# Folding the third hop's weights into the first hop's product, and turning its sums on VectorE

## Chip, cores and metric

The program runs on one core of a Trainium2 chip. A core has TensorE (PE in the profile; its weight loads are PEld), VectorE (DVE), ScalarE (ACT), GpSimd (POOL), SyncE (SP, which here only issues transfers) and 16 DMA engines. The metric is the device time of one execution in microseconds. The median of three runs of the kernel before is 697.6 us (697.42 to 697.65).

## What is computed

A stack of four graph layers works on node vectors `x` of 3327 nodes by 64 features and one dense-stored adjacency `adj` of 3327 x 3327, all float32. Each layer is `x = x + layer(relu(layernorm(x)), adj)`. Cut to what matters here:

```python
# layer 0: two gated cells, each m = adj @ (h @ W), then gates (sigmoid, tanh)      hops 0, 1
# layer 1: a rank-weighted mask of adj times (h @ weight) + bias                     hop 2
# layer 2: w = adj * adj; three hops with a dense layer each                         hops 3, 4, 5
for W, b in ((W0, b0), (W1, b1), (W2, b2)):
    x = w @ x
    x = x @ W.T + b
# layer 3: twice x = tanh(concat(adj @ x, x) @ W[k])                                 hops 6, 7
```

So there are eight products with an N x N matrix. The change concerns layer 2. A product from the right with the small matrices commutes with the products with `w` from the left, so `W0`, `W1` and `W2` may be applied at any one of the three hops, as long as each bias goes through the matrices that follow it: `b0` is still multiplied by `w` twice, `b1` once.

## The kernel before

**Tiling.** The nodes are padded to 26 blocks of 128. Blocks are paired (block b and block 13 + b stand in the two 64-row halves), which gives 13 pairs in four chunks: chunks 0, 1 and 2 have three pairs (384 columns), chunk 3 has four (512). Chunks 0 and 1 are group 0; chunks 2 and 3 are group 1. An adjacency tile is one source block (26 of them) by one group. A unit of work is one hop, one chunk and one tile: two matmuls into the two halves of a PSUM bank (L613). The records show four instructions for each, since a float32 product is recorded as two.

**Order of the hops.** `joint(g, k, ...)` at L661 writes down the order of units for hop k and hop k+1 of one group, so that a tile loaded once serves both. The call `joint(1, 4)` does hops 4 and 5 of group 1, then `joint(0, 5)` hops 5 and 6 of group 0, then `joint(1, 6)`. Within one, tiles of the other group's nodes come first; hop k+1 follows hop k by four tiles (`later=4`). The group's own tiles come next. The last `sweep` of them are done for the first chunk completely, then for the second, so that the first chunk's sums are finished early. Then the waiting tiles of hop k+1 are done, then hop k+1 over the first chunk's own sources for both chunks, then over the second chunk's own sources for the first chunk, and for the second.

**Tasks.** What follows a chunk's last unit (evacuation, dense layer, layernorm) is a Python generator, `after_k`. Nothing in it is dynamic on the chip: while the program is written out, every unit "spends" a time (0.645 for a 384-column chunk, 0.86 for 512, L617), and a generator that has yielded a time is continued when that time is spent. So a `yield` sets only after which unit the next instructions are put into the engines' queues. `begin` for a chunk first runs the chunk's old task to its end (`finish`, L372), and a unit that reads a node vector which its task has not yet set runs that task to its end (L603). The task of loading and folding constants, `more_constants`, ends with `fold_hops` (L228), which multiplies `W0` and `W1` into one matrix (`product(1, 2)`).

**Hop 5 before.** `after_5` (L1013) copies the sums to SBUF (`evacuate`: VectorE for even chunks, ScalarE for odd), multiplies them with `W2` on TensorE (`dense_to_nodes`, which at the same time brings them from feature layout to node layout), adds the result to `x` from PSUM (`residual`), normalises (`layernorm_relu`), and after 8.0 writes the transposed vector into `both[c]` with 16 VectorE transposes (`transpose_on_vector`) for the concatenation of hop 6. `b2` was added to `x` long before, by `add_row(c, 2)` at the end of `after_2`. Hop 4 already has no dense product: `sums_to_nodes` (L813) adds a bias column on ScalarE and turns the sums with 16 VectorE transposes of 32-row blocks.

**Squares.** Hops 3 to 5 need `adj * adj`. In `joint(0, 5)` the tile itself is still needed by hop 6, so each unit squares its part into a separate half slot, three units ahead (`expand`, L490). `square` (L444) chooses the engine: ScalarE, except that every third square goes to VectorE when no chunk has a task alive.

**After hop 6.** `after_6` (L1025) copies the sums into the free halves of `both[c]`, one half on ScalarE (L830), one on VectorE (L834), and 1.3 later TensorE multiplies `both` with layer 3's weights (`stacked_to_nodes`, L780).

Of the kernel before, what the change touches and what calls it, by code (L numbers as in the profile page):

```python
# [9 lines left out]
F32 = mybir.dt.float32  # L10
# [3 lines left out]
ALU = mybir.AluOpType  # L14
# [30 lines left out]
N, D = 3327, 64  # L45
P = 128
# [9 lines left out]
GROUPS = [(0, 1), (2, 3)]  # L56
# [9 lines left out]
WL1, WL2, WL3 = 14, 15, 18  # L66
# [25 lines left out]
def upper(n):  # L92
    return slice(n * D, (n + 1) * D)
# [3 lines left out]
def kernel(  # L97
# [9 lines left out]
    nc = tc.nc  # L107
# [3 lines left out]
    work = ctx.enter_context(tc.tile_pool(name="work", bufs=4))  # L111
# [11 lines left out]
    bd = const.tile([P, 4, P], F32, name="bd")  # L123
# [7 lines left out]
    brow = const.tile([P, 4, D], F32, name="brow")  # L131
    hopcol = const.tile([P, 2], F32, name="hopcol")
    ident = const.tile([P, P], F32, name="ident")
    make_identity(nc, ident)
    tri = const.tile([P, P], BF16, name="tri")
    behind = const.tile([P, NQ - 1 + D], BF16, name="behind")
# [77 lines left out]
    def product(i, j):  # L214

        n, ps = take()
        mm(ps[:, :P], bd[:, i, :], ident)
        tr = work.tile([P, P], F32, name="t2")
        nc.scalar.copy(tr, ps[:, :P])
        give(n)  # L220
        yield 1.0
        n, ps = take()
        mm(ps[:, :P], tr, bd[:, j, :])
        nc.scalar.copy(bd[:, i, :], ps[:, :P])
        give(n)
        yield 1.0

    def fold_hops():  # L228

        i, ps = take()  # L230
        for n in range(3):
            for h in range(2):
                nc.tensor.matmul(ps[upper(h), n * P:(n + 1) * P], brow[:, n], ident, start=True, stop=True)
        cols = work.tile([P, CWM], F32, name="t2")
        nc.scalar.copy(cols[:, :3 * P], ps[:, :3 * P])
        give(i)
        yield 1.0

        i, ps = take()
        mm(ps[:, :D], cols[:, :P], bd[:, 2, :D])  # L240
        nc.vector.tensor_copy(brow[:, 0], ps[:, :D])
        nc.vector.tensor_copy(hopcol[:, 0:1], cols[:, P:P + 1])
        give(i)
        yield 1.0
        yield from product(1, 2)

    def more_constants():
# [54 lines left out]
    def blocks(c):  # L302
        return CH[c][1] - CH[c][0]

    def width(c):
        return blocks(c) * P

    def mm(out, lhsT, rhs, start=True, stop=True):


        for h in range(2):
            hs = slice(h * D, (h + 1) * D)
            nc.tensor.matmul(out[hs], lhsT[:, hs], rhs, start=start, stop=stop)  # L313
# [8 lines left out]
    def take(sums=False, either=True):  # L322


        either = either and not sums
        pool = idle_sums if sums else idle_temps
        if either and idle_sums and (not pool or released[idle_sums[0]] < released[pool[0]]):
            pool = idle_sums
        for c in list(tasks):
            if not pool and c not in running:  # L330
                advance(c)
        i = pool.popleft()
        return i, banks[i]

    def give(i):
        released[i] = max(released) + 1
        (idle_sums if i < 4 else idle_temps).append(i)

    def nodes(c):

        return feat.tile([P, blocks(c), 2, D], F32, name=f"y{c}")

    def flat(t):
        return t.rearrange("p b s d -> p b (s d)")
# [4 lines left out]
    def xchunk(c):  # L349
        return xs[:, CH[c][0]:CH[c][1]]  # L350
# [8 lines left out]
    def advance(c):  # L359
        running.add(c)  # L360
        try:
            tasks[c][1] = next(tasks[c][0])
        except StopIteration:
            del tasks[c]
        running.discard(c)
# [6 lines left out]
    def finish(c):  # L372
        while c in tasks:
            advance(c)
# [14 lines left out]
    y = [[None] * NC for _ in range(8)]  # L389
# [233 lines left out]
    def put(k, c, t):  # L623
        units.append((k, c, t))
        if k == COUNT or KIND[k] != RANKED or c == GROUPS[t.g][0]:
            t.uses += 1
# [34 lines left out]
    def joint(g, k, sweep, later, keep, lag=None):  # L661


        a, b = GROUPS[g]
        in_place = KIND[k] != PLAIN and KIND[k + 1] == SQUARED
        early = (KIND[k], KIND[k + 1]) == (PLAIN, RANKED)
        waiting = deque()
        counting = Counting(g, lag)

        def both(t):  # L670
            for c in (a, b):
                put(k, c, t)
            if lag is not None:
                counting.add(t)

        def second(n):
            for _ in range(n):
                if waiting:
                    t = waiting.popleft()
                    for c in (a, b):  # L680
                        put(k + 1, c, t)

        for q in sources_of(*GROUPS[1 - g]):
            t = Tile(q, g, in_place, early)
            both(t)
            waiting.append(t)
            if len(waiting) > later:
                second(1)
        own = [[Tile(q, g, in_place, early) for q in sources_of(c)] for c in (a, b)]
        all_own = own[0] + own[1]  # L690
        for n, t in enumerate(all_own[:-sweep]):
            both(t)
            second(len(waiting) + n + 1 > later if early else min(2, len(waiting) - keep))
        counting.rest()
        for c in (a, b):
            for t in all_own[-sweep:]:
                put(k, c, t)
                if lag is not None and c == a:
                    counting.add(t)
            if KIND[k] == RANKED:  # L700
                units.append((k, c, SPECIAL))
        counting.rest()
        second(len(waiting))
        for t in own[0]:
            for c in (a, b):
                put(k + 1, c, t)
        for c in (a, b):
            for t in own[1]:
                put(k + 1, c, t)
            if KIND[k + 1] == RANKED:  # L710
                units.append((k + 1, c, SPECIAL))
# [44 lines left out]
    def evacuate(acc, c, busy=False):  # L756
        m = work.tile([P, CWM], F32, name="t2")[:, :width(c)]
        if c % 2 or busy:
            nc.scalar.copy(m, acc[0][1][:, :width(c)])
        else:  # L760
            nc.vector.tensor_copy(m, acc[0][1][:, :width(c)])  # L761
        give(acc[0][0])
        return m

    def dense_to_nodes(ft, w, c):

        i, ps = take()
        v = view(ps, c)
        for b in range(blocks(c)):
            mm(v[:, b, :], ft[:, b * P:(b + 1) * P], bd[:, w - WL1, :])  # L770
        return i, v
# [38 lines left out]
                if q % 2:  # L810
                    yield 1.5

    def sums_to_nodes(acc, c, bias):  # L813

        m = work.tile([P, CWM], F32, name="t2")[:, :width(c)]
        nc.scalar.activation(m, acc[0][1][:, :width(c)], AF.Identity, bias=hopcol[:, bias:bias + 1])  # L816
        give(acc[0][0])
        yield 0.8
        v = m.rearrange("p (b q n) -> p b q n", q=4, n=32)
        yk = nodes(c)  # L820
        for s in range(2):
            for f in range(2):
                at = s * D + f * 32
                for q in range(4):
                    nc.vector.transpose(yk[q * 32:(q + 1) * 32, :, s, f * 32:(f + 1) * 32], v[at:at + 32, :, q])  # L825
                yield 1.2
        return yk
# [33 lines left out]
    def residual(v, c, relu=False):  # L861
        if relu:
            nc.vector.scalar_tensor_tensor(flat(xchunk(c)), v[1], 0.0, flat(xchunk(c)), op0=ALU.max, op1=ALU.add)
        else:
            nc.vector.tensor_tensor(flat(xchunk(c)), flat(xchunk(c)), v[1], ALU.add)  # L865
        give(v[0])

    def add_row(c, i):

        n = 2 * blocks(c)  # L870
        nc.vector.tensor_tensor(groups(xchunk(c)), groups(xchunk(c)),
                                brow[:, i:i + 1, :].to_broadcast([P, n, D]), ALU.add)
# [113 lines left out]
    def after_2(c, acc):  # L986
        m = evacuate(acc, c)
        yield 1.4
        v = dense_to_nodes(m, WL1, c)
        yield 1.2  # L990
        residual(v, c)
        yk = nodes(c)
        yield from layernorm_relu(yk, c, squares_on_scalar=c in GROUPS[0])
        y[3][c] = yk
        yield 15.0
        add_row(c, 2)

    def after_3(c, acc):
        m = evacuate(acc, c)
# [11 lines left out]
        y[5][c] = yield from sums_to_nodes(acc, c, 0)  # L1011

    def after_5(c, acc):  # L1013
        m = evacuate(acc, c)
        yield 0.8
        v = dense_to_nodes(m, WL2 + 2, c)
        yield 0.8
        residual(v, c)
        yk = nodes(c)
        yield from layernorm_relu(yk, c)  # L1020
        y[6][c] = yk
        yield 8.0
        yield from transpose_on_vector(yk, c)
# [31 lines left out]
    joint(1, 2, sweep=6, later=6, keep=1)  # L1055
    joint(0, 3, sweep=8, later=4, keep=4)
    joint(1, 4, sweep=8, later=4, keep=4)
    joint(0, 5, sweep=8, later=4, keep=4)
    joint(1, 6, sweep=8, later=4, keep=4)
    alone(0, 7, sweep=6, parts=True)  # L1060

# [55 lines left out]
```

## Time and profile before

| | us |
|---|---|
| median of three runs | 697.6 |
| the profiled execution's own time | 697.73 |
| its span, first to last instruction | 695.7 |
| TensorE busy | 681.0 (98%) |
| VectorE busy | 355.3 (51%) |
| ScalarE busy | 274.3 (39%) |
| GpSimd busy | 77.8 (11%) |

Times in the trace count from the start of the span. In a row of a group, the number behind "x" is how many instructions it has, then come their busy time in us and the mean of one in ns, then the idle time of the engine ahead of them and what ended it. In the chain, a row is start, length and the engine with the written tile and the line. In a timeline, a row is start, length, engine, line, operation, output and input with shapes, and in brackets the idle time ahead of it.

The 16 DMA engines moved 201.31 MB in the span, 289 GB/s on average.

### The profile page before, as it was taken

The page shows a single profiled execution, that of the slowest core. Times are in us where ns is not written, and L with a number is a line of the kernel's source. Part 1 is how long each engine was busy: PE and PEld are TensorE (multiplying, and loading weights), DVE is VectorE, ACT ScalarE, POOL GpSimd, SP SyncE. Part 2 cuts the span into 40 slices and gives each one's busy share as a digit, 9 for nine tenths or more (in the row PEclk, how much of TensorE's full clock was granted, in tenths as well). Part 3 has the DMA queues.
Part 4 walks back from the last instruction along what each step waited for, and adds up shares of the span by engine and source line. Part 5 has one row for each costly group of instructions (what it writes and reads, how often), then busy time and mean ns, then how long its engine had stood idle before and what let it go on. Part 6 is the DMA issues. An engine that isn't in the chain of part 4 may idle for free.

```text
span 695.7 us, 12589 instructions
## 1 busy us (share of the span) xinstructions
PE 681.0 (98%) x5072; PEld 380.4 (55%) x5072; DVE 355.3 (51%) x772; ACT 274.3 (39%) x426; POOL 77.8 (11%) x114
## 2 busy tenths in 40 slices
PE   7899999999999999999999999999999999999997
PEld 4686667645566785556444444343344444344587
DVE  5946745755997899757341106325271565005101
ACT  1013000403147878888998107722176500000101
POOL 5300000002480414111100000000000000000000
PEclk9999999999999999999999999999999999999999
DMA  9999998099879921792899569954997399917991
GB/s 341 401 400 406 403 407 274 1 349 389 277 242 376 317 96 60 259 316 80 311 361 351 206 216 409 404 227 131 396 370 264 110 399 405 405 75 268 404 403 65
DMA packets 68693, 201.31 MB, mean 289 GB/s; under 512 B 7244, under 2 KB 8372, under 8 KB 68636
## 3 DMA queue, kind: packets, MB, share of 16 engines
q1 hardware_dynamic: 65724, 199.08, 76.9%
q10 hardware_dynamic: 736, 1.23, 0.5%
q8 instruction: 40, 0.66, 0.4%
q0 software_dynamic: 2176, 0.20, 0.2%
q14 instruction: 17, 0.14, 0.0%
HBM read 199.45 MB, written 0.85 MB: 288 GB/s over the span
## 4 chain that ended last, share of the span: by engine, by line
PE 58%; DVE 1%; ACT 0%; POOL 0%; issue 0%; DVEq 0%; ACTq 0%; POOLq 0%
PE sum L613 54%; PE temp L313 3%; PE temp L780 1%; ACT e L529 0%; POOL st L854 0%; DVE both L834 0%; DVE e L527 0%; PE sum L313 0%; ACT both L830 0%; DVE y L858 0%; DVE y L850 0%; DVE t L845 0%; DVE st L851 0%; DVE st L843 0%; DVE xs L865 0%
## 5 line engine op out<-in xcount | busy, mean ns | idle before, releaser
L613 PE MATMUL sum<-adj,y 128*64 128x384 f32 (+3 forms) x3016 | 535.4, 501 | 1.5 <-DVE y L858 0.7
L613 PEld LDWEIGHTS sum<-adj,y 128*64 128x64 f32 x3016 | 248.8, 137 | 230.5 <-issue 196.9
L446 ACT ACTIVATE adj<-adj 128x768 f32<-128x768 f32 (+1 forms) x176 | 144.4, 892 | 45.9 <-PE sum L613 23.0
L472 DVE TENSOR_SCALAR adj<-adj 128x768 bf16<-128x768 f32 (+3 forms) x208 | 114.0, 597 | 32.6 <-PE temp L548 24.7
L613 PE MATMUL sum<-e,both 128*64 128x384 bf16 (+1 forms) x624 | 74.0, 339 | 0.5 <-DVE e L527 0.5
L529 ACT ACTIVATE e<-temp,bitsb 128x384 int16<-128x384 f32 (+1 forms) x120 | 67.8, 607 | 14.9 <-PE temp L313 9.1
L830 ACT COPY both<-sum 64x384 f32<-64x384 f32 (+3 forms) x17 | 8.1, 478 | 148.2 <-PE sum L613 148.2
L834 DVE COPY both<-sum 64x384 f32<-64x384 f32 (+3 forms) x13 | 7.3, 561 | 99.5 <-ACT both L830 98.9
L448 DVE TENSOR_TENSOR adj<-adj 128x768 f32<-128x768 f32 (+1 forms) x32 | 30.6, 1004 | 51.9 <-DMA adj<-in_adjT 33.1
L854 POOL TENSOR_TENSOR st<-st,mhalf 128x6 f32<-128x6 f32 (+1 forms) x16 | 24.9, 1553 | 287.8 <-DVE st L852 287.8
L313 PE MATMUL temp<-adj,tri 128*64 128x384 bf16 (+1 forms) x332 | 51.7, 341 | 1.3 <-ACT e L529 0.8
L613 PEld LDWEIGHTS <-both 128*64 128x64 bf16 x624 | 41.9, 110 | 18.3 <-issue 6.5
L477 POOL DMA_DIRECT2D adj<-totals x52 | 33.6, 648 | 52.6 <-PE temp L313 41.7
L313 PEld LDWEIGHTS <-tri 128*64 128x64 bf16 x416 | 29.2, 110 | 17.3 <-issue 9.8
L527 DVE TENSOR_SCALAR e<-temp 128x384 int16<-128x384 f32 (+1 forms) x46 | 28.3, 615 | 20.0 <-PE temp L313 9.6
L809 DVE STREAM_TRANSPOSE both<-y 32x96 f32<-32x96 f32 (+1 forms) x128 | 35.6, 278 | 2.9
L548 PE MATMUL temp<-adj,behind 128*64 128x384 bf16 x208 | 33.8, 340 | 2.8 <-DVE adj L472 2.6
L825 DVE STREAM_TRANSPOSE y<-t 32x96 f32<-32x96 f32 (+1 forms) x64 | 17.8, 278 | 24.7 <-ACT t L816 23.9
L548 PEld LDWEIGHTS <-behind 128*64 128x64 bf16 x208 | 20.8, 110 | 17.4 <-issue 13.5
L761 DVE COPY t<-sum 128x384 f32<-128x384 f32 x6 | 3.3, 555 | 35.7 <-PE sum L613 35.7
L186 ACT COPY t<-temp 128x128 f32<-128x128 f32 x1 | 0.3, 266 | 48.2 <-PE temp L184 48.2
L570 POOL MEMSET adj<- 128x768 f32 (+1 forms) x2 | 1.6, 800 | 133.2 <-PE sum L613 133.2
(132 smaller groups left out, 353.8 us busy)
## 6 DMA issues: line engine op xcount, KB each, us to landing
adj<-in_adjT SPq DMA_DIRECT2D x130, 768.0 KB, 9.0
adj<-in_adjT SPq DMA_DIRECT2D x104, 896.0 KB, 12.0
xs<-in_x ACTq DMA_DIRECT2D x1, 448.0 KB
adj<-totals POOLq DMA_DIRECT2D x26, 3.0 KB, 4.9
adj<-totals POOLq DMA_DIRECT2D x26, 3.5 KB, 2.3
out<-xs ACTq DMA_DIRECT2D x1, 256.0 KB
xs<-in_x SPq DMA_DIRECT2D x1, 192.0 KB
xs<-in_x ACTq DMA_DIRECT2D x1, 192.0 KB, 3.3
```

The costliest lines, as they stand in the source:

```text
L313: nc.tensor.matmul(out[hs], lhsT[:, hs], rhs, start=start, stop=stop)
L446: nc.scalar.activation(sq, v, AF.Square)
L448: nc.vector.tensor_tensor(sq, v, v, ALU.mult)
L472: nc.vector.tensor_scalar(t.mask.view[:rows, half], t.view()[:rows, half], 0.0, None, op0=ALU.not_equal)
L477: nc.gpsimd.dma_start(out=t.mask.view[P - 1:P], in_=totals[t.g][t.q:t.q + D + 1:D, :])
L527: nc.vector.tensor_scalar(wide[:, s], ps[:, :w], BITS, 0.0, op0=ALU.add, op1=ALU.max)
L529: nc.scalar.activation(wide[:, s], ps[:, :w], AF.Relu, bias=bitsb)
L548: nc.tensor.matmul(counts[c][1][s * D:(s + 1) * D, :w], behind[:, NQ - 1 - t.q:NQ - 1 - t.q + D], t.mask.view[:, s, t.cols(c)], start=firs ...
L613: nc.tensor.matmul(acc[h][1][h * D:(h + 1) * D, :w], yq[h], rhs[h], start=first and n == 0, stop=last and n == len(terms) - 1)
L809: nc.vector.transpose(to[at:at + 32, :, q], h[q * 32:(q + 1) * 32, :, s, f * 32:(f + 1) * 32])
L825: nc.vector.transpose(yk[q * 32:(q + 1) * 32, :, s, f * 32:(f + 1) * 32], v[at:at + 32, :, q])
L854: nc.gpsimd.tensor_tensor(st[:, 3, :n], st[:, 2, :n], mhalf[:, :n], ALU.pow)
```

## The change

The three matrices of layer 2 are folded into one at the start, `W0.T @ W1.T @ W2.T` (a second `product`), which hop 3's dense product applies. `b0`'s row goes through `W1` and `W2`, `b1`'s column through `W2`, and `b2` becomes a column of its own. Hop 5 then needs no product: like hop 4, it adds a bias column on ScalarE and turns the sums on VectorE, and adds the result to `x` from SBUF. `add_row` for `b2` goes. In hop 5 the second chunk of a group issues its turns only once the first chunk's normalised vector is set (the loop with `yield 0.3`, at most 50 times). In `joint(0, 5)` the sweep is 12 instead of 8: all twelve own tiles of group 0 are done for chunk 0 first, then for chunk 1.

```diff
         mm(ps[:, :D], cols[:, :P], bd[:, 2, :D])
+        mm(ps[:, D:D + 1], bd[:, 3, :], cols[:, P:P + 1])
         nc.vector.tensor_copy(brow[:, 0], ps[:, :D])
-        nc.vector.tensor_copy(hopcol[:, 0:1], cols[:, P:P + 1])
+        nc.vector.tensor_copy(hopcol[:, 0:1], ps[:, D:D + 1])
+        nc.vector.tensor_copy(hopcol[:, 1:2], cols[:, 2 * P:2 * P + 1])
         give(i)
         yield 1.0
+        i, ps = take()
+        for h in range(2):
+            nc.tensor.matmul(ps[upper(h), :P], brow[:, 0], ident, start=True, stop=True)
+        col = work.tile([P, P], F32, name="t2")
+        nc.scalar.copy(col, ps[:, :P])
+        give(i)
+        yield 1.0
+        i, ps = take()
+        mm(ps[:, :D], col, bd[:, 3, :D])
+        nc.vector.tensor_copy(brow[:, 0], ps[:, :D])
+        give(i)
+        yield 1.0
+        yield from product(2, 3)
         yield from product(1, 2)
...
-    def sums_to_nodes(acc, c, bias):
+    def sums_to_nodes(acc, c, bias, behind=None):
...
         yield 0.8
+        for _ in range(50):
+            if behind in (None, c) or y[6][behind] is not None:
+                break
+            yield 0.3
+        else:
+            finish(behind)
         v = m.rearrange("p (b q n) -> p b q n", q=4, n=32)
...
         y[3][c] = yk
-        yield 15.0
-        add_row(c, 2)
...
-        m = evacuate(acc, c)
-        yield 0.8
-        v = dense_to_nodes(m, WL2 + 2, c)
-        yield 0.8
-        residual(v, c)
-        yk = nodes(c)
+        yk = yield from sums_to_nodes(acc, c, 1, behind=GROUPS[c // 2][0])
+        nc.vector.tensor_tensor(flat(xchunk(c)), flat(xchunk(c)), flat(yk), ALU.add)
         yield from layernorm_relu(yk, c)
...
-    joint(0, 5, sweep=8, later=4, keep=4)
+    joint(0, 5, sweep=12, later=4, keep=4)
```

## Prediction

> **What bounds the kernel now.** I read the page first (busy times, slices of the span), then the groups of instructions with their shapes kept apart.
>
> ```profile
> span 695.7 us, 12589 instructions
> ...
> PE 681.0 (98%) x5072; PEld 380.4 (55%) x5072; DVE 355.3 (51%) x772; ACT 274.3 (39%) x426; POOL 77.8 (11%) x114
> ...
> PE   7899999999999999999999999999999999999997
> ...
> L825 DVE STREAM_TRANSPOSE y<-t 32x96 f32<-32x96 f32 x48 | 12.9, 270 | 22.1 <-ACT t L816 21.4
> ...
> L313 PE MATMUL temp<-bd,t 128*64 128x128 f32 x148 | 10.2, 273 | 0.0
> ```
>
> TensorE is never idle for long: from 340 to 650 us the table by stage shows it busy 10.00 of every 10 us. So a matmul removed there is worth its full length, and a wait added there costs its full length. VectorE is half idle on average, but the average does not decide; what decides is what stands in its queue when TensorE next needs it. The second view is therefore the chain in order of time (start, us, what) around hop 5 of both groups:
>
> ```profile
> 497.61 0.68 PE temp L313 x12
> ...
> 505.59 0.87 PE temp L313 x16
> 506.46 41.28 PE sum L613 x256
> 547.74 0.66 PE temp L313 x12
> 548.39 5.16 PE sum L613 x32
> 553.55 0.66 PE temp L313 x12
> ...
> 571.62 0.70 PE temp L780 x24
> ```
>
> The four L313 pieces are the products with hop 5's weights that the change removes (52 of the 148 records of the group above, 13 blocks by 4). A "unit" below is one chunk times one adjacency tile, four matmul records: 41.28 / 64 = 0.645 us for a 384-wide chunk; a 512-wide one takes 0.86. The third view is the timeline of VectorE, then of ScalarE, behind that point:
>
> ```profile
> 560.02 5.99 DVE L809 STREAM_TRANSPOSE both<-y 32x96 f32<-32x96 f32 x20
> 570.24 0.56 DVE L834 COPY both<-sum 64x384 f32<-64x384 f32 x1 [4.24 <-ACT both L830]
> 570.83 3.57 DVE L809 STREAM_TRANSPOSE both<-y 32x96 f32<-32x96 f32 x12
> 574.81 0.56 DVE L834 COPY both<-sum 64x384 f32<-64x384 f32 x1 [0.41 <-ACT both L830]
> ...
> 545.25 5.47 ACT L446 ACTIVATE adj<-adj 128x768 f32<-128x768 f32 x7 [0.83 <-ACT adj L446]
> ```
>
> The reader is to see that the copy of chunk 0's hop-6 sums (570.24) found VectorE idle for 4.24 us, and that 20 of the 32 feature transposes stood in front of it, 12 behind.
>
> [...] 12 transposes, ready since 560, ran only after the copy at 570.24 that waited for TensorE. The forecast goes by this. [...] a chunk needs 16 of them, 4.53 us in the trace (470.35 to 474.88), where TensorE's product took 0.66; so I price the change by queue time.
>
> **Part by part.**
> *Removed on the path:* the four products, 0.68 + 0.87 + 0.66 + 0.66 = 2.87 us. Four `add_row` of 0.55 to 0.68 us (VectorE, at 281.5, 288.2, 334.1, 351.6) lie beside a TensorE that is busy without a gap there: nothing. The hop-2 tasks end 15 us sooner, so VectorE may take a third of the squares from 341 on, where ScalarE is busy 10.00 of 10; but no unit of TensorE waits for ScalarE there, so that is no gain either.
>
> *Fold.* Added to TensorE near 162 us: a one-column product (bounded by the 64-column one, 0.11), two transposes (0.22), a 64-column product (0.11), `product(2, 3)` (2 x 0.22, as 164.36 to 164.58): 0.88. Later TensorE waits 0.31 us at 178.84 for VectorE (L921), whose chain runs from 173.46 unbroken; the two added steps after that start hide in it. Against that, copies may queue on ScalarE beside the tanh L915, which waits for VectorE: 0 to 0.7. I take +0.7 (0.5 to 1.3). The 0.36 us of VectorE copies meet its idle 1.42 us before 170.02.
>
> *Chunks 2 and 3 (group 1).* The ScalarE activation (0.58; 0.69 at 512) replaces a copy. Chunk 2: 16 turns 4.53, then add to normalised vector 5.39 (498.33 to 503.72); ready 0.6 + 4.5 + 5.4 = 10.6 us after its sums; hop 6 wants it after 8 units of 0.86 and 10 of 0.645, 13.3 us: hidden. Chunk 3 is held, ready some 15 us after its own sums; wanted after 34 units, 21.9: hidden. But hop 5 of group 0 opens with ten units without hop-6 units between. ScalarE squares one in 0.767 us (5.37 / 7 at 504.87), units 4 to 10 after the 0.69 activation: done at about 6.0 us, TensorE wants the tenth at 5.8. The removed 0.87 us product was its cover. Cost 0.3.
>
> *Sweep 12.* Number units from hop 5's start in group 0. Own tiles begin at unit 49 (time s). Chunk 0's sums now end with unit 60 (64 before), chunk 1's with 72; 73 to 80 finish the waiting hop-6 tiles; 81 to 92 read chunk 0's vector, 93 to 104 chunk 1's, and chunk 0's hop-6 sums end with 98. A task's `yield` counts whole units: 0.8 and 1.2 are 2, 1.5 is 3, 8.0 is 13. Chunk 3's task now lives until unit 52, and while a task lives all squares go to ScalarE: 11 in a row from s - 1.87 at 0.775 us end at s + 6.66, TensorE wants that one at s + 6.45. With two more squares ahead of it, chunk 0's activation starts at about s + 8.2, and chunk 1's last square is some 0.95 us late.
>
> *The hold, and what it queues.* Chunk 0's vector is set at unit 79 (60 + 2 + 4 x 2 + 3 x 3). Chunk 1 is held until then; its turns are issued at 79, 81, 83, 85, its normalisation would end at unit 96. Unit 93 needs it, so `finish(1)` runs the whole task there, with all 16 feature transposes of chunk 1, which before came at 98 and later. The copy of chunk 0's hop-6 sums (unit 98) then stands behind 16 + 12 transposes. (The same count gives 16 + 4 ahead of the copy for the kernel before: the x20 row.) VectorE's time, from s: activation 8.2 + 0.58; turns 4.53; chunk 0's chain 5.39; chunk 1's turns 4.53; its add to L852 3.33; pow and L858 2.06 (four transposes fit under the pow); 28 transposes at 0.30 = 8.4; copy 0.56; hand-overs 0.3: s + 37.9. TensorE, never waiting, would want it after unit 101, at s + 53 x 0.645 = s + 34.2. So 3.7 us are lost, including the 0.95. A ScalarE without lag gives 3.3; a pow of 1.8 us, as at 180.89, gives 4.1. The turns are bounded by 16 x 0.270 = 4.3 and by 16 x 0.30 = 4.8 each time. I take 3.6. After it VectorE has caught up; nothing else waits.
>
> *DMA.* The last own tile is wanted 4 units sooner. In the stage table DMA falls to nothing after 541, 4.6 us behind the start of the own tiles (536.3 there); its square starts at s + 5.2 or later: free.
>
> Sum: -2.87 + 0.7 + 0.3 + 3.6 = +1.7. The profiled run took 697.73 us (span 695.7), 0.13 over the median 697.6. So 699.4 on the profiled run, 699.3 on the median; between the two I say 699.4.
>
> **Rivals.**
> 1. *Queue stall as above:* 699.4; its own range 698.7 to 700.5 (stall 3.3 to 4.1, fold 0.5 to 1.3). For it: the count reproduces the x20/x12 split. Chance 0.60.
> 2. *Not slower: the early finish doesn't block.* If chunk 1's vector is set before unit 93, its 16 transposes (4.8 us) fall behind the copy, which is then on time; only the ScalarE lag is left: 697.6 - 2.87 + 0.7 + 0.3 + 0.95 = 696.7. It decides at three units (1.9 us): the hold would have to end at unit 76 instead of 79. Against it: the count. 0.13.
> 3. *The saving carries all:* also no ScalarE lag, because VectorE takes its third of the squares: 697.6 - 2.87 + 0.7 = 695.4. Against it: chunk 3's task lives into the own tiles. 0.09.
> 4. *A late tile:* the last own tile's load waits for a slot freed later than now; its issue-to-landing of 4.9 us starts some 2.5 us later, past its square, moving the whole VectorE chain by 1.5 or more: 701. Against it: own units free no slot in either order. 0.12.
> 5. *The fold stalls more,* each of its five new steps waiting behind gate work on ScalarE: +1.5, 700.9. 0.06.
>
> **Numbers.** A measurement can tell about 0.2%, 1.4 us: below 696.2 faster, above 699.0 slower. Case 1 falls above with 0.78 of its weight (0.47), with 4 and most of 5: slower 0.64. Same: the rest of 1 and case 2, 0.26. Faster: 0.10. Range 696.5 to 701.2, leaving about 0.1 on either side.
>
> **What would show it.** Right: 52 fewer records of the products for hop 5; 128 turns in the group that now has 64; TensorE waiting 2 to 4 us near 570, ahead of the stacked product (now L780), for the VectorE copy of `both` (now L834); in the VectorE timeline a run of 28 transposes ahead of it; small TensorE waits on squares near 510 and 550. Wrong: no idle at L780 (case 2 or 3); a wait on the load of `adj` near 540 (case 4); idle near 162 to 178 (case 5). The price of the turns (0.283 us each) fails if they wait for each other longer when chunk 1's follow chunk 0's chain without a gap.

## The result

The changed kernel takes 699.31 us (median of seven runs, 698.99 to 700.9); the kernel before took 697.6 in runs between them (697.42 to 697.82). The ratio is 1.0033, interval [1.0023, 1.0042]: slower by 1.7 us. The forecast was 699.4. Three of the seven runs stand at 700.83 to 700.9 with a mean granted clock of 0.998, four at 698.99 to 699.31 with 1.000; where the upper level comes from is taken up with the last experiment.

The profiled execution took 699.31. The page of the changed kernel, in the parts that answer to those shown of before:

```profile
span 697.4 us, 12588 instructions
...
PE 680.6 (98%) x5040; PEld 374.4 (54%) x5040; DVE 372.0 (53%) x834; ACT 274.0 (39%) x429; POOL 77.6 (11%) x114
...
PE   7899999999999999999999999999999989999997
...
L846 DVE STREAM_TRANSPOSE y<-t 32x96 f32<-32x96 f32 (+1 forms) x128 | 35.6, 278 | 41.1 <-ACT t L831 39.4
```

TensorE's busy time hardly moved (681.0 to 680.6), although four products of 2.87 us left it: the fold put some 0.88 back, and 0.90 in which TensorE only follows ScalarE's squares (below) counts as busy; the other 0.7 I can't name. The turns are 128 now. One slice of the row PE has fallen from 9 to 8, the 33rd, which covers 558 to 575 us. The wait list of TensorE names what is in it (us in total, times, longest):

```profile
PE temp L795 <- DVE both L855: 2.3, 1, 2.3
...
PE sum L628 <- ACT e L544: 0.5, 1, 0.5
```

(Line numbers have moved: L780 is L795, L834 is L855, L830 is L851, L809 is L824, L825 is L846, L613 is L628, L858 is L879, L854 is L875, L446 is L461, L529 is L544.) The timeline of VectorE ahead of that wait (start, us, then the idle time before in brackets):

```profile
554.52 4.51 DVE L846 STREAM_TRANSPOSE y<-t 32x96 f32<-32x96 f32 x16
...
562.42 1.12 DVE L824 STREAM_TRANSPOSE both<-y 32x96 f32<-32x96 f32 x4
563.89 0.56 DVE L879 SCALAR_TENSOR_TENSOR y<-t,st 128x384 f32<-128x384 f32 x1 [0.35 <-POOL st L875]
564.49 8.10 DVE L824 STREAM_TRANSPOSE both<-y 32x96 f32<-32x96 f32 x28
572.62 0.56 DVE L855 COPY both<-sum 64x384 f32<-64x384 f32 x1
```

and TensorE in the same stretch:

```profile
570.68 0.28 PE L795 MATMUL temp<-w,both 128*64 128x64 f32 x4
573.24 0.80 PE L795 MATMUL temp<-w,both 128*64 128x64 f32 x20 [2.27 <-DVE both L855]
```

Before the change, the copy of chunk 0's hop-6 sums found VectorE idle and ran at 570.24. Now VectorE works without a gap through 28 feature transposes, first the 16 of chunk 1 and then the last 12 of chunk 0, and the copy comes at 572.62. The product that needs it has begun with its first part and then stands for 2.27 us.

The account along TensorE, from the same events of the two traces, is short (the sums' end is read at the start of the instruction that takes them out of PSUM):

| event | before | after | moved by |
|---|---|---|---|
| chunk 2's hop-5 sums are taken | 496.80 | 497.99 | +1.19 |
| chunk 3's hop-5 sums are taken | 504.39 | 504.86 | +0.47 |
| chunk 1's hop-5 sums are taken | 552.31 | 552.19 | -0.12 |
| chunk 1's stacked product starts | 575.76 | 577.48 | +1.72 |
| VectorE's last step in the chain | 692.72 | 694.43 | +1.71 |

Of the first 1.19, 0.07 was there before the fold begins; 1.12 is the fold. The next step falls by 0.72, one product. Between rows two and four three products leave (0.87 + 0.66 + 0.66 = 2.19), yet the kernel loses 1.25 there: 3.44 us are new.

Of these, 0.90 lie in the 72 units of hop 5: the first starts at 504.64, and the hop-6 unit behind the last one at 551.98, where 72 x 0.645 gives 551.08. TensorE's wait list doesn't have them, because what waits is the load of its weights (PEld). Between 503 and 553 us the list of PEld has, before and after,

```profile
PEld sum L613 <- ACT adj L446: 1.1, 6, 0.2
PEld sum L628 <- ACT adj L461: 9.5, 24, 0.5
```

and its timeline in the changed kernel shows units that come 0.73 us apart, as fast as ScalarE squares, rather than 0.645:

```profile
508.52 0.20 PEld L628 LDWEIGHTS sum<-adj,y 128*64 128x64 f32 x4 [0.51 <-ACT adj L461]
509.26 0.20 PEld L628 LDWEIGHTS sum<-adj,y 128*64 128x64 f32 x4 [0.54 <-ACT adj L461]
509.99 0.20 PEld L628 LDWEIGHTS sum<-adj,y 128*64 128x64 f32 x4 [0.54 <-ACT adj L461]
```

Most of such a wait lies under the matmuls of the unit before: of the 9.5 us in the list TensorE loses 0.90. The lag grows by 0.33 in the ten opening units, by 0.17 in units 57 to 59 and by 0.40 in units 68 to 72. The wait above is 2.27 more. Another 0.22 goes with it: the product is cut in two, and its parts take 0.28 + 0.80 us where the whole took 0.87. That leaves 0.05.

### The profile page after: what moved, and what is told of

Same layout as the page of the kernel before. It is cut to its first block, busy times and chain, and to the rows that moved or that the text cites. A ratio compares the mean times of both kernels' runs of the same rounds, so it can differ in the third digit from the quotient of the medians.

```text
span 697.4 us, 12588 instructions
## 1 busy us (share of the span) xinstructions
PE 680.6 (98%) x5040; PEld 374.4 (54%) x5040; DVE 372.0 (53%) x834; ACT 274.0 (39%) x429; POOL 77.6 (11%) x114
## 4 chain that ended last, share of the span: by engine, by line
PE 54%; DVE 4%; ACT 1%; POOL 0%; issue 0%; POOLq 0%; DVEq 0%; ACTq 0%
PE sum L628 51%; PE temp L328 2%; DVE y L846 1%; DVE both L824 1%; PE temp L795 1%; POOL st L875 0%; ACT e L544 0%; DVE t L866 0%; DVE y L871 0%; DVE y L879 0%; DVE st L864 0%; DVE st L872 0%; POOLq L1127 0%; DVE both L855 0%; DVE xs L1034 0%
## 5 line engine op out<-in xcount | busy, mean ns | idle before, releaser
L628 PE MATMUL sum<-adj,y 128*64 128x384 f32 (+3 forms) x3016 | 536.4, 501 | 1.1 <-DVE y L879 0.6
L628 PEld LDWEIGHTS sum<-adj,y 128*64 128x64 f32 x3016 | 245.1, 137 | 235.8 <-issue 194.4
L461 ACT ACTIVATE adj<-adj 128x768 f32<-128x768 f32 (+1 forms) x174 | 142.0, 889 | 22.4 <-DMA adj<-in_adjT 11.9
L628 PE MATMUL sum<-e,both 128*64 128x384 bf16 (+1 forms) x624 | 73.8, 339 | 1.0 <-ACT e L544 0.5
L544 ACT ACTIVATE e<-temp,bitsb 128x384 int16<-128x384 f32 (+1 forms) x120 | 67.8, 606 | 15.4 <-PE temp L328 9.6
L851 ACT COPY both<-sum 64x384 f32<-64x384 f32 (+3 forms) x17 | 8.1, 478 | 147.3 <-PE sum L628 147.3
L855 DVE COPY both<-sum 64x384 f32<-64x384 f32 (+3 forms) x13 | 7.3, 561 | 99.3 <-ACT both L851 98.8
L463 DVE TENSOR_TENSOR adj<-adj 128x768 f32<-128x768 f32 (+1 forms) x34 | 32.9, 1015 | 47.7 <-DMA adj<-in_adjT 32.9
L846 DVE STREAM_TRANSPOSE y<-t 32x96 f32<-32x96 f32 (+1 forms) x128 | 35.6, 278 | 41.1 <-ACT t L831 39.4
L875 POOL TENSOR_TENSOR st<-st,mhalf 128x6 f32<-128x6 f32 (+1 forms) x16 | 24.8, 1553 | 292.4 <-DVE st L873 292.4
L628 PEld LDWEIGHTS <-both 128*64 128x64 bf16 x624 | 41.7, 110 | 19.2 <-issue 7.6
L824 DVE STREAM_TRANSPOSE both<-y 32x96 f32<-32x96 f32 (+1 forms) x128 | 35.6, 278 | 2.0
L831 ACT ACTIVATE t<-sum,hopcol 128x384 f32<-128x384 f32 (+1 forms) x8 | 4.8, 606 | 51.9 <-PE sum L628 51.7
```

Of the source, the lines that this page charges most:

```text
L461: nc.scalar.activation(sq, v, AF.Square)
L463: nc.vector.tensor_tensor(sq, v, v, ALU.mult)
L544: nc.scalar.activation(wide[:, s], ps[:, :w], AF.Relu, bias=bitsb)
L628: nc.tensor.matmul(acc[h][1][h * D:(h + 1) * D, :w], yq[h], rhs[h], start=first and n == 0, stop=last and n == len(terms) - 1)
L824: nc.vector.transpose(to[at:at + 32, :, q], h[q * 32:(q + 1) * 32, :, s, f * 32:(f + 1) * 32])
L875: nc.gpsimd.tensor_tensor(st[:, 3, :n], st[:, 2, :n], mhalf[:, :n], ALU.pow)
```

## The experiments

Each kernel ran in turn with the kernel before on one chip. The theory is the prediction's first case (VectorE's queue, filled by the early finish of chunk 1's task); the rivals change from one experiment to the next.

**Moving the 16 transposes behind the copy.** A unit that needs a vector now continues the task only as far as the vector, rather than to its end. In the queues of the engines this changes one thing: chunk 1's 16 feature transposes come after chunk 0's copy.

```diff
-            if y[k][cs] is None:
-                finish(cs)
+            while y[k][cs] is None:
+                advance(cs)
```

> The changed kernel, but a unit of TensorE that needs a vector which its task has not set yet runs that task only up to the vector, not to its end. In the queues this moves one thing alone: the 16 feature transposes of chunk 1 come behind VectorE's copy of chunk 0's hop-6 sums instead of ahead of it. My theory (the copy stood behind 16 + 12 transposes): TensorE's wait of 2.3 us at the stacked product of chunk 0 goes, 699.3 falls to about 697.0. Rival (VectorE is simply short of time there, whatever the order): the wait comes back at chunk 1's stacked product, whose copy now stands behind the 16, and the time stays within 0.5 us of 699.3.

Measured: 697.34 us (697.24 to 697.71) beside 697.69 before, ratio 0.9996 [0.9988, 1.0004]. The timeline of VectorE in this kernel:

```profile
564.69 3.52 DVE L824 STREAM_TRANSPOSE both<-y 32x96 f32<-32x96 f32 x12
569.66 0.56 DVE L855 COPY both<-sum 64x384 f32<-64x384 f32 x1 [1.46 <-ACT both L851]
570.25 4.79 DVE L824 STREAM_TRANSPOSE both<-y 32x96 f32<-32x96 f32 x16
575.07 0.56 DVE L855 COPY both<-sum 64x384 f32<-64x384 f32 x1
```

The copy again finds VectorE idle, for 1.46 us, and the wait at chunk 0's product is gone. The order of VectorE's instructions is otherwise that of the changed kernel, from the first to the last. The 16 transposes are now ahead of chunk 1's copy, and a wait of 0.39 us stands at chunk 1's product; the rival is right by that much, and it is why 697.0 was not reached. So the price of the early finish is 699.31 - 697.34 = 1.97 us; 2.27 - 0.39 = 1.88 of it is in the wait list. The change's loss against before, 1.7 us, is no more than this: it hangs on the place of sixteen transposes that do not belong to the change.

**Taking away the hold.** Chunk 1's turns may then stand ahead of chunk 0's chain.

```diff
-        yk = yield from sums_to_nodes(acc, c, 1, behind=GROUPS[c // 2][0])
+        yk = yield from sums_to_nodes(acc, c, 1)
```

> The changed kernel without the hold: chunk 1's turns (and chunk 3's) are issued as soon as its sums are in SBUF. The sweep of 12 stays. My theory: the vector of chunk 1 is then set at unit 91, before unit 93 asks for it, nothing is run early, and the 2.3 us wait goes; chunk 3's task also ends before the own tiles, VectorE takes a third of their squares again, and the 0.8 us by which ScalarE is late go too: about 696.2. Rival (the hold is what keeps chunk 0's vector on time; without it chunk 1's turns stand ahead of chunk 0's last step): TensorE waits 1 us or more at the first unit that reads chunk 0's vector, 698 or more.

Measured: 698.48 us (698.32 to 699.18), ratio 1.0012 [1.0005, 1.0018]. The stall at chunk 0's product went, as expected, but the time did not fall to 696.2. Of ScalarE's lag only the 0.17 in units 57 to 59 went; the other 0.73 stayed. The expectation regarded group 0 alone. In group 1 TensorE now waits:

```profile
512.57 2.80 PE L628 MATMUL sum<-adj,y 128*64 128x384 f32 x16 [1.08 <-DVE y L879]
```

The timeline of VectorE in this kernel shows why. Chunk 3's turns fill the 1.5 us in which chunk 2's chain waits for GpSimd's pow, and run on past it:

```profile
508.14 3.79 DVE L846 STREAM_TRANSPOSE y<-t 32x128 f32<-32x128 f32 x12
511.96 0.56 DVE L879 SCALAR_TENSOR_TENSOR y<-t,st 128x384 f32<-128x384 f32 x1
```

In the changed kernel this last step of chunk 2 ran at 507.98, four microseconds earlier, and nobody waited for it. So the hold pays for itself in group 1 with 1.1 us there. In group 0 it leads to the early finish, which costs 1.97. Both are effects of one line, and the prediction had a price for the second alone. A wait of 0.4 us at chunk 1's product is also in this kernel.

**The sweep of 8 kept, the hold too.** Here chunk 0's sums end four units later, and its whole chain with them.

```diff
-    joint(0, 5, sweep=12, later=4, keep=4)
+    joint(0, 5, sweep=8, later=4, keep=4)
```

> The changed kernel with the sweep of 8 as before the change; the hold stays. My theory: chunk 0's sums end 4 units (2.6 us) later, its vector is asked for before it is due, its whole task runs early and its 16 feature transposes stand ahead of chunk 1's turns; chunk 1's vector is about 7 us late at the first unit that reads it, in place of the 3.3 us that the changed kernel loses: about 703. Rival (the longer sweep itself is what costs, by squares or loads): the time is at or under 699.3.

Measured: 705.9 us (705.43 to 706.14), ratio 1.0117 [1.0104, 1.0131]. The order on VectorE was the expected one and TensorE waited 6.54 us for chunk 1's vector. But the kernel is 6.6 us slower than the changed one, not 3.7. The timeline of TensorE in this kernel, and below it the table by stage (window; its length; busy us and records of PE, PEld, DVE, ACT and POOL; granted clock; DMA share; GB/s):

```profile
571.80 8.32 PE L628 MATMUL sum<-adj,y 128*64 128x384 f32 x36 [6.54 <-DVE y L879]
```

```profile
571.80:574.00 2.20, 2.19 (x8) 0.98 (x10) 1.98 (x8) 0.00 (x0) 0.00 (x0) 0.50 1.02 404
574.00:576.00 2.00, 2.00 (x8) 0.71 (x8) 1.78 (x8) 0.00 (x0) 0.00 (x0) 0.50 1.03 407
576.00:578.00 2.00, 2.00 (x12) 0.77 (x10) 0.53 (x2) 0.00 (x0) 0.00 (x0) 0.88 1.03 407
578.00:580.00 2.00, 2.00 (x16) 0.88 (x14) 0.56 (x1) 0.47 (x1) 0.00 (x0) 1.00 1.01 401
```

After the wait the granted clock is 0.50 in the first two stretches, 4.2 us, and 0.88 in the third: 36 records take 8.32 us, where 36 x 0.161 = 5.8 would do. That is 2.5 of the missing 2.9 us. For the change it follows that the longer sweep is no ornament: with the hold and the early finish in place it is worth 6.6 us. What it is worth without the early finish was not run.

**The fold alone.** The kernel before with the fold's steps put in and their results used by nothing: it measures the fold's time and no other part of the change.

> The kernel before, with the added products of the fold computed and not used (in the same number of steps, written to places that nothing reads later); hop 5 still has its own product. This measures the fold by itself. My step priced it at +0.7 (0.5 to 1.3); the trace of the changed kernel, 1.2 us later than the one before by the time of hop 3, 0.08 of it from the start, says +1.1: 698.3 to 698.7. Rival (the fold hides in waits of TensorE that are there anyway): under +0.3.

Measured: 699.01 us (698.89 to 699.18) beside 697.69, ratio 1.002 [1.0012, 1.0028]: +1.3, above both. Inside the span the expected +1.1 is right: from 203 us on, TensorE is 1.12 us later than in the kernel before, as in the changed kernel. The rest lies outside the span, for in this kernel the time is 2.3 us longer than the span, in the kernel before 2.0 and in the changed one 1.9; why is not shown. Of the 1.12, 0.50 is there at 181 us: the five added steps were counted at 0.88, and the wait of 0.31 for L921 is gone. The other 0.62 comes with a wait that the kernel before does not have, in the timeline of TensorE 40 us behind the fold:

```profile
201.35 0.68 PE L628 MATMUL sum<-e,both 128*64 128x384 bf16 x6 [0.51 <-ACT e L544]
```

The changed kernel has the same wait at 201.42. So it belongs to the fold; how the fold brings it about is not shown.

**The copy on ScalarE.** Chunk 0's second half copy is taken off VectorE; the 28 transposes stay.

```diff
-        evacuate_stacked(acc, c)
+        evacuate_stacked(acc, c, on_scalar=c == 0)
```

> The changed kernel with chunk 0's hop-6 copy taken by ScalarE, so that nothing of that copy stands in VectorE's queue; the 28 transposes stay as they are. My theory: the stacked product needs chunk 0's own last 12 transposes too, which stand behind chunk 1's 16, so only the copy's 0.57 us is saved: a wait of about 1.7 us, 698.7. Rival (the copy alone is what is late): the wait goes, 697.0.

Measured: 698.58 us (698.43 to 699.13), ratio 1.0013 [1.0007, 1.002]. The wait list of this kernel has, in place of the 2.3 us for the copy:

```profile
PE temp L795 <- DVE both L824: 1.4, 2, 0.8
```

The copy was not what was late: the product of chunk 0 needs chunk 0's own last 12 transposes, and these still stand behind the 16 of chunk 1. TensorE's wait falls from 2.27 to 1.4 us, the time by 0.7.

**A wait with nothing of the change in it.** The kernel before, with a small copy out of chunk 0's hop-6 sums and nine transposes of it ahead of the copy. They are added work which nothing uses.

```diff
     def after_6(c, acc):
+        if c == 0:
+            idle = work.tile([P, CWM], F32, name="t2")
+            nc.vector.tensor_copy(idle[0:32, 96:192], acc[0][1][0:32, 96:192])
+            for _ in range(9):
+                nc.vector.transpose(...)     # operands left out
         evacuate_stacked(acc, c)
```

> The kernel before with nothing of the change, but a copy of 32 x 96 and 9 transposes of unused data put ahead of chunk 0's hop-6 copy in VectorE's queue: about 2.8 us of VectorE, 0.65 of it slack, so TensorE waits some 2.1 us at chunk 0's stacked product. What it tells apart: three of seven runs of the changed kernel took 700.9 at a mean granted clock of 0.998, where the others took 699.2 at 1.000. If a wait of this length by itself brings TensorE's clock down in some runs, this kernel takes 699.8 in some and 701.4 in others. If the second level belongs to something else of the change, all runs take 699.8.

Measured: 699.5 us (699.2 to 699.83), ratio 1.0024 [1.0016, 1.0033]. The wait was 1.59 us, not the 2.1 that were expected, and the time went up by 1.9: at this point of the kernel a wait of TensorE costs its full length and 0.3 more, of which 0.2 is again the product cut in two (0.28 + 0.80 us for 0.87). All eleven runs have a clock of 0.999 or 1.000; none stands on a second level. But the wait came out shorter than the 2.27 us of the changed kernel, so this run alone doesn't decide between the two.

**The squares of the own tiles.** The first experiment's kernel, with `square` told to regard only the tasks of group 0 while it squares group 0's own tiles. Chunk 3's task, still alive, then no longer keeps VectorE out.

```diff
-    def square(sq, v, turn):
-        if turn % 3 or any(ch in tasks or (2, ch) in sums for ch in range(NC)):
+    def square(sq, v, turn, chunks=range(NC)):
+        if turn % 3 or any(ch in tasks or (2, ch) in sums for ch in chunks):
...
-            square(wide, t.view(c), t.q + c)
+            own = chunk_of(t.q % NB) in GROUPS[t.g]
+            square(wide, t.view(c), t.q + c, GROUPS[t.g] if own else range(NC))
```

> As the version that runs a late task only up to its vector (697.34), and besides the squares of group 0's own tiles go to VectorE by their old third as long as no task of group 0 itself lives, whether or not chunk 3's task does. My theory: of the 0.9 us by which TensorE falls behind ScalarE in hop 5's own tiles, the half before chunk 0's sums goes: 696.9. Rival (those 0.9 us are not ScalarE's): 697.3.

Measured: 697.14 us (696.84 to 697.87), ratio 0.9992 [0.9985, 0.9998]. The gain over the kernel it was built on is 0.2 us (0.13, if each is compared with the kernel before that ran beside it), too small for these intervals to tell from the rival's 697.3. The trace tells: the lag behind 72 units is 0.73 us rather than 0.90, and what went is all of the 0.17 in units 57 to 59. The lag is ScalarE's; the expectation took half of it to lie there, and most lies elsewhere.

**The version that beats both.** The same, with chunk 1's copy after hop 6 on ScalarE, where the 16 transposes now stand ahead of it on VectorE.

```diff
-        evacuate_stacked(acc, c)
+        evacuate_stacked(acc, c, on_scalar=c == GROUPS[0][1])
```

> The same, and chunk 1's hop-6 copy on ScalarE, which removes the wait of 0.39 us that the version with the late task run up to its vector had at chunk 1's stacked product: 696.5, about 1.2 us under the kernel before.

Measured: 696.56 us (696.44 to 696.98) beside 697.62, ratio 0.9984 [0.9977, 0.9991]: 2.75 us below the changed kernel, 1.06 below the one before. After 480 us its wait list for TensorE holds a single row:

```profile
PE sum L629 <- DVE both L856: 0.2, 1, 0.2
```

The kernel before has this wait as well. The sum closes: the removal of four products is worth 2.87 us, the fold takes 1.1, the lag of the squares, 0.73 in this trace, is left, and 2.87 - 1.1 - 0.73 = 1.04 for the measured 1.06.

**A longer bare wait.** The upper level of the changed kernel (1.7 us more, clock 0.998) was still without a cause. This is the earlier kernel with 12 transposes for 9, again unused work.

> The kernel before, with a copy of a 32x96 piece out of chunk 0's hop-6 sums and 12 transposes of it (not used by anything) ahead of chunk 0's copy after hop 6, in place of the 9 of the earlier run; so TensorE waits about 2.4 us for that copy (1.6 + 3 x 0.27) and nothing else of the change is in it. Theory (the wait itself lowers the granted clock in some executions[...]): most executions at 697.6 + 1.9 + 0.8 = 700.3, and some at about 701.9 with a mean clock of 0.998. Rival (the second level of the changed kernel comes from something else in it): all executions at 700.3, clock 1.000.

Measured: 701.37 us (700.9 to 702.56), ratio 1.0052 [1.0038, 1.0066]. One of the five runs has a clock of 0.998 and 702.56; it is the profiled one. Its timeline of TensorE, then its table by stage (stretches of 2 us, columns as above):

```profile
574.11 0.80 PE L780 MATMUL temp<-w,both 128*64 128x64 f32 x20 [2.49 <-DVE both L834]
574.74 5.30 PE L613 MATMUL sum<-adj,y 128*64 128x384 f32 x20
```

```profile
572.00:574.00 2.00, 0.00 (x0) 0.00 (x0) 1.83 (x6) 0.00 (x0) 0.00 (x0) 1.00 1.02 405
574.00:576.00 2.00, 1.89 (x26) 1.27 (x28) 1.78 (x8) 0.49 (x1) 0.00 (x0) 0.75 1.01 401
576.00:578.00 2.00, 2.00 (x8) 0.73 (x6) 1.50 (x6) 0.00 (x0) 0.00 (x0) 0.50 1.06 413
578.00:580.00 2.00, 2.00 (x16) 0.76 (x14) 0.89 (x3) 0.47 (x1) 0.00 (x0) 0.89 1.01 398
580.00:582.00 2.00, 2.00 (x34) 1.15 (x32) 1.91 (x8) 0.49 (x1) 0.00 (x0) 1.00 1.03 405
```

Behind the wait of 2.49 us the granted clock is 0.75, 0.50 and 0.89 in three stretches and 1.00 again in the next; the 20 records behind it take 5.30 us where they took 3.61 with the nine transposes: 1.69 us, the height of the changed kernel's upper level. None of the change is in this kernel, so the lower clock, here in one execution of five, needs nothing of it. That the upper level of the changed kernel is this same lower clock is concluded from its mean clock and its height, since the profiled execution was one of the lower level. Not all is settled: the four other runs, at clock 1.000, lie at 700.9 to 701.4, 0.6 to 1.1 above the 700.3 that the wait accounts for; they left no trace, and why is not shown. One of 62 runs of the kernel before took 699.82 at clock 1.000 too, where no other took over 698.05; so a run can lose two microseconds by something that these numbers don't name.

## Why the prediction was right

The time is right (699.31 for 699.4), and so is the mechanism. Two terms of the sum were mis-sized, the fold by 0.4 too little and the stall by 0.5 too much. That they cancel, so that the sum came within 0.1, is luck.

*Removed products, -2.87.* Right where it can be read alone: 0.72 between chunk 2's and chunk 3's sums for a product of 0.68.

*The fold, +0.7 (0.5 to 1.3).* Mis-sized: in the traces of the changed kernel and of the fold alone it is 1.12. The step beside the fold is right: 0.88 added, less the hidden part, is 0.57, and 0.50 is measured. What failed is that the prediction looked for waits near 162 to 178 us alone. The 0.62 at 200 us come later, with a wait (0.51 us at 201.42) that the kernel before does not have. The upper end of the range covered it; the value chosen in it did not.

*Ten opening units, +0.3.* Right: 0.33, with the weight loads waiting for ScalarE's squares as was said.

*The hold's stall, +3.6, of it 0.95 lag of ScalarE.* Mechanism right to the count: the early finish, 16 + 12 transposes ahead of the copy, the wait at chunk 0's stacked product. The size is the wait of 2.27, the 0.22 of the product cut in two and 0.57 of lag in the own tiles: 3.06, below the 3.3 to 4.1 given. The lag was taken 0.38 too high. On VectorE the 28 transposes took 8.10 us for the 8.4 that were allowed, and the 0.3 for hand-overs does not appear. That VectorE runs its instructions in the order of their issue carried this step, and the rows show it: here the copy runs at 572.62, behind 28 transposes, though ScalarE took its half of the same sums at 568.96; in the first experiment it runs at 569.66, behind 12, and the 16 follow it at 570.25.

*DMA, free.* Right; there is no wait for a load of `adj` in TensorE's list.

*The hidden chains of chunks 2 and 3.* Right for the kernel as it is, but why they are hidden was not seen: without the hold, chunk 2's is not (1.1 us).

*The rivals.* Case 2, in which the early finish doesn't block, is the first experiment's kernel: 696.7 was said and 697.34 measured. With the fold at 1.1 it would have said 697.1; the rest is the small wait at chunk 1's product, less the lag that was taken too high. Case 3, no lag at all, is nearly the last version: 695.4 said, 695.8 with the fold at 1.1, and 696.5 with the lag of 0.73 that this version still has, for 696.56 measured. A late tile (case 4) did not occur. Of case 5, a fold that stalls more, the kernel had about the half (1.1, between 0.7 and 1.5), though not near 162 us where that case looked for it.

*What the prediction lacked.* A second level. It priced a wait of TensorE by its length alone. At the stacked product the waits of 1.59 and 2.27 us each cost 0.2 us more than their length (0.28 + 0.80 us for 0.87), and three runs of seven came out 1.7 us higher. That the median fell on the lower level is luck too; with four of the seven on the upper one it would have been 700.8.

## What to carry to other kernels

When a product is moved from a busy engine to an idle one, count what stands in the idle engine's queue at the moment the busy one next needs it: here VectorE was half idle, and the loss came from 16 transposes, not part of the change, that were put into its queue too early. A helper that runs a task to its end because one value is needed issues everything else in the task as well; run it only as far as the value. Look at the waits of TensorE's weight loads as well as at its own: 0.90 us of lag stood in the first list alone. And a wait of TensorE can cost more than its length in some executions of a kernel and not in others: with the 2.27 us here, three of seven took another 1.7 us.

## What the runs showed of the hardware

The longest wait of TensorE near the change in a kernel's profile, and the runs of that kernel with a lower mean granted clock:

| longest wait | runs with the mean clock at 0.998 or below | cost beyond the wait |
|---|---|---|
| 0.8 to 1.6 us (three kernels) | 0 of 53 | |
| 2.3 us (the changed kernel) | 3 of 7 | 1.7 us |
| 2.5 us (longer bare wait) | 1 of 5 | 1.7 us in its trace |
| 6.5 us (sweep of 8) | 4 of 4 | 2.5 us |

The first row's kernels are the one without the hold (1.1 us), the one with the copy on ScalarE (two waits, 0.8 the longer) and the nine transposes.

In the changed kernel's profiled execution, one of the lower level, the granted clock stays at 1.00 around the wait of 2.27 us, which ends at 573.24:

```profile
570.00:572.00 2.00, 0.97 (x10) 0.43 (x6) 1.80 (x7) 0.00 (x0) 0.00 (x0) 1.00 1.03 407
572.00:574.00 2.00, 0.77 (x22) 0.77 (x24) 1.10 (x3) 0.00 (x0) 0.00 (x0) 1.00 1.03 405
574.00:576.00 2.00, 2.00 (x16) 0.88 (x14) 0.00 (x0) 0.49 (x1) 0.00 (x0) 1.00 1.02 405
576.00:578.00 2.00, 2.00 (x32) 1.12 (x30) 1.40 (x5) 0.47 (x1) 0.00 (x0) 1.00 1.03 407
```

Behind the 2.49 us of the longer bare wait it falls to 0.50, and so it does behind the 6.54 us of the sweep of 8 (both tables above). Why the same wait lowers the clock in some executions of a kernel and not in others is not shown by these runs.
